# Even and odd blocks in place of first and second half in a block-Toeplitz convolution, with one PSUM pool for both of its steps

## The chip, the core and the metric

The kernel runs on one core of a Trainium2 chip. The metric is the device time of one execution in microseconds. Three executions of the kernel before are at hand; their median is 13,579.16 us. About 0.2% (27 us) is what a measurement of this kernel can tell from no change.

## The reference, cut to what matters

Two layers with residuals on x of 32 images, 128 channels and 32 x 32 pixels. The change lies in the first layer, in the part between the encoder and the first Gelu:

```python
u = _gn(x).reshape(Bsz, S, L)                       # B=32, S=128, L=1024
h = jnp.einsum('bdl,de->ble', u, W_enc) + b_enc     # 1024 hidden channels
...
K = 2.0 * jnp.einsum('dn,dnl->dl', Cc * Bd, vand).real     # 64 taps a channel
z = jnp.swapaxes(h, 1, 2)
y = jnp.fft.irfft(jnp.fft.rfft(z, n=n_fft) * jnp.fft.rfft(K, n=n_fft), n=n_fft)[..., :L]
y = y + D[:, None] * z
y = jax.nn.gelu(jnp.swapaxes(y, 1, 2))
...
```

So each of 1024 channels of each image is convolved along its 1024 positions with its own 64 taps, causally; the skip term D goes into tap 0. What follows (a gated linear unit, a layer norm, a decoder, then a deformable convolution as the second layer) is computed by a main block that the change leaves alone.

## The kernel before, in words

Four steps run one after the other: a table of the taps (`ssm_kernel_table`), the convolution (`ssm_convolution`), the main block, and a rare fallback. The main block takes some 12.1 ms of the 13.6. Everything here is in `ssm_convolution`, which ends at about 1450 us of the profile.

The convolution runs as eight passes `k`, each over 128 hidden channels: first `encode(k)`, then `convolve(k, z)`. Within them the instructions of each engine run in the order in which the program writes them (`tc.manual_schedule()`, L343), so the order of the Python statements is the order of each engine's queue.

*Encode.* For each of the 32 images, `image(b, u)` (L218) multiplies the image's eight blocks of 128 positions with 128 columns of `W_enc` (L223). Four blocks make a group `g`, and fill one tile of one PSUM bank from the pool `psz`, which has two tiles (L203). VectorE adds the bias and writes the result as `z[g]` (L227), with the block `j` and the image `b` innermost, so that 4 blocks x 32 images are 128 columns. Group 0 holds blocks 0 to 3, group 1 blocks 4 to 7, each in the order `ORDER` = 0, 2, 1, 3. In pass 0 the images come from x and go through a group norm in five steps (`group_norm_steps`, L161 to L180), whose two small matmuls (L170, L175) write into one tile of the pool `psy`; the normalised images are stored to `u_d`. In later passes they are loaded from there (L236; 512 KB each, five buffers).

*Convolve.* It goes over 16 groups of eight channels (`CG`). Each loads a Toeplitz table `toe` of 192 columns a channel (L281, 768 KB, three buffers, on SyncE's queue). For `q` in 0 and 1 (four channels each) and for `i` in 0 and 1 (the group of blocks) a tile of two banks is taken from `psy`, which has three (L204), and four matmuls fill it (L299). Each gives 192 columns a channel: 128 belong to a block itself, and 64 (`RW`) are the overlap that belongs to the next block. ScalarE copies the overlaps out of PSUM (L307, tile `t`). VectorE adds them to the blocks that they belong to (`carry`, L311): in the order 0, 2, 1, 3 the overlap of blocks 0 and 2 goes onto 1 and 3 (64 partitions), that of block 1 onto 2 (32 partitions), and in the second group that of block 3 onto block 4 (32 partitions, from the tile `last` of the first group). That is two additions for the first group and three for the second.

The Gelu of a tile (L320) is not issued at once. It is put on a list `waiting`, and `finish()` (L271) issues what is on the list after the copy and the additions of the tile that follows. The order on ScalarE is therefore: copy of tile n, Gelu of tile n-1, copy of tile n+1, Gelu of tile n. The Gelu is the last to read a tile and so lets it go. It writes `yo` (six buffers, two a group of channels). After both `q` the eight stores of a group of channels go onto the same list (L332): 128 KB each, issued on GpSimd's queue.

[...]

Of the kernel before, what the change touches and what calls it, by code (L numbers as in the profile page):

```python
# [7 lines left out]
F32 = mybir.dt.float32  # L8
AF = mybir.ActivationFunctionType
# [5 lines left out]
P = 128  # L15
# [10 lines left out]
TW = 192  # L26
# [3 lines left out]
CG = 8  # L30
# [130 lines left out]
def group_norm_steps(nc, pool, pm, gavg, eps, xt, out):  # L161


    s = pool.tile([P, 1], F32, tag="gn_s", name="gn_s")
    nm = pool.tile([P, 1], F32, tag="gn_m", name="gn_m")
    ss = pool.tile([P, 1], F32, tag="gn_ss", name="gn_ss")
    r = pool.tile([P, 1], F32, tag="gn_r", name="gn_r")
    nc.scalar.activation(out, xt, AF.Identity, accum_out=s)
    yield
    nc.tensor.matmul(pm[:, 0:1], gavg, s, start=True, stop=True)  # L170
    yield
    nc.scalar.mul(nm, pm[:, 0:1], -1.0)
    nc.scalar.activation(out, xt, AF.Square, bias=nm, accum_out=ss)
    yield
    nc.tensor.matmul(pm[:, 1:2], gavg, ss, start=True, stop=True)  # L175
    yield
    nc.scalar.activation(r, pm[:, 1:2], AF.Sqrt, bias=eps)
    nc.vector.reciprocal(r, r)
    nc.vector.tensor_scalar(out, xt, nm, r, op0=ALU.add, op1=ALU.mult)
    yield  # L180


def ssm_convolution(nc, tc, const, ins, x, u_d, kp_d, y_d):
# [12 lines left out]
    with tc.tile_pool(name="cvt", bufs=3) as tp, tc.tile_pool(  # L196
        name="cvz", bufs=1
    ) as zp, tc.tile_pool(name="cv1", bufs=1) as one, tc.tile_pool(
        name="cvu", bufs=5
    ) as up, tc.tile_pool(name="cvy", bufs=6) as yp, tc.tile_pool(  # L200
        name="cvg", bufs=4
    ) as gp, tc.tile_pool(
        name="cv_psz", bufs=2, space=PSUM  # L203
    ) as psz, tc.tile_pool(name="cv_psy", bufs=3, space=PSUM) as psy:  # L204
        w_enc = one.tile([P, D], F32, tag="w_enc", name="w_enc")
        nc.sync.dma_start(w_enc, ins["W_enc"])
        b_enc = one.tile([P, D], F32, tag="b_enc", name="b_enc")
        nc.sync.dma_start(b_enc, ins["b_enc_row"].to_broadcast([P, D]))

        def encode(k):  # L210

            z = [
                pool.tile([P, P, NB, B], F32, tag=f"z{g}", name=f"z_{k}_{g}")
                for g, pool in enumerate((one, zp))
            ]
            bias = b_enc[:, k * P : (k + 1) * P]

            def image(b, u):  # L218
                for g in range(2):
                    ps = psz.tile([P, NB, P], F32, tag="ps", name=f"psz_{k}_{b}_{g}")  # L220
                    for j in range(NB):
                        lo = (NB * g + ORDER[j]) * P
                        nc.tensor.matmul(  # L223
                            ps[:, j, :], u[:, lo : lo + P], w_enc[:, k * P : (k + 1) * P],
                            start=True, stop=True,
                        )
                    nc.vector.tensor_add(  # L227
                        z[g][:, :, :, b].rearrange("p d j -> p j d"),
                        ps,
                        bias[:, None, :].to_broadcast([P, NB, P]),  # L230
                    )

            if k > 0:
                for b in range(B):
                    u = up.tile([P, L], F32, tag="u", name=f"u_{k}_{b}")
                    nc.sync.dma_start(u, u_d[b])  # L236
                    image(b, u)
                return z


            running = {}

            def step(b):
                if b in running:
                    next(running[b][1])

            for t in range(B + 3):
                step(t - 2)
                if t - 2 in running:
                    nc.scalar.dma_start(u_d[t - 2], running[t - 2][0])  # L250
                step(t - 1)
                if t < B:
                    u = up.tile([P, L], F32, tag="u", name=f"u_{k}_{t}")
                    xt = yp.tile([P, L], F32, tag="yo", name=f"xt_{t}")
                    nc.sync.dma_start(xt, x[t])
                    pm = psy.tile([P, 2, 512], F32, tag="ps", name=f"gn_ps_{t}")
                    running[t] = u, group_norm_steps(
                        nc, gp, pm[:, 0, :2], const["gavg"], const["eps"], xt, u
                    )
                    step(t)  # L260
                if t >= 3:
                    image(t - 3, running.pop(t - 3)[0])
                step(t - 1)
                step(t)
            return z

        def convolve(k, z):
            rows = [t.rearrange("p d j b -> p d (j b)") for t in z]
            waiting = []

            def finish():  # L271
                for work in waiting:
                    work()
                waiting.clear()

            for g in range(P // CG):
                d0 = k * P + g * CG
                toe = tp.tile([P, CG, TW], F32, tag="toe", name=f"toe_{d0}")
                table = kp_d[d0 : d0 + CG, 0:TW]

                nc.sync.dma_start(  # L281
                    toe,
                    bass.AP(
                        tensor=table.tensor,
                        offset=table.offset,
                        ap=[[1, P], [KPW, CG], [1, TW]],
                    ),
                )
                yo = [
                    yp.tile([P, CG, P], F32, tag="yo", name=f"yo_{d0}_{i}") for i in range(2)  # L290
                ]
                for q in range(CG // QC):
                    c0 = q * QC
                    last = None
                    for i in range(2):
                        ps = psy.tile([P, 2, 512], F32, tag="ps", name=f"psy_{d0}_{q}_{i}")
                        ps = ps[:, :, : 2 * TW].rearrange("p h (c n) -> p h c n", c=2)
                        for c in range(QC):
                            nc.tensor.matmul(  # L299
                                ps[:, c // 2, c % 2, :],  # L300
                                rows[i][:, g * CG + c0 + c, :],
                                toe[:, c0 + c, :],
                                start=True,
                                stop=True,
                            )
                        over = tp.tile([P, 2, 2, RW], F32, tag=f"t{i}", name=f"t_{d0}_{q}_{i}")
                        nc.scalar.copy(over, ps[:, :, :, :RW])  # L307

                        def carry(to, rows, src):
                            own = ps[to : to + rows, :, :, P:TW]  # L310
                            nc.vector.tensor_add(own, own, src)  # L311

                        carry(64, 64, over[0:64])
                        carry(32, 32, over[64:96])
                        if i > 0:
                            carry(0, 32, last[96:P])
                        finish()

                        def gelu(to=yo[i][:, c0 : c0 + QC, :], ps=ps):
                            nc.scalar.activation(  # L320
                                to.rearrange("p (h c) l -> p h c l", c=2),
                                ps[:, :, :, RW:TW][:, :, :, ::-1],
                                AF.Gelu_apprx_tanh,
                            )

                        waiting.append(gelu)
                        last = over

                def store(yo=yo, d0=d0):
                    for i in range(2):  # L330
                        for j in range(NB):
                            nc.gpsimd.dma_start(  # L332
                                y_d[d0 : d0 + CG, :, i * NB + ORDER[j], :].rearrange(
                                    "d b l -> b d l"
                                ),
                                yo[i][j * B : (j + 1) * B],
                            )

                waiting.append(store)
            finish()  # L340


        with tc.manual_schedule():  # L343
            for k in range(KD):
                convolve(k, encode(k))


def deformable_general(nc, tc, const, ins, x1_d, out, image):
# [7 lines left out]
    with tc.tile_pool(name="gdf1", bufs=1) as one, tc.tile_pool(  # L356
# [27 lines left out]
        def prepare(b):  # L384
# [2 lines left out]
            nc.sync.dma_start(xt, x1_d[bass.ds(image, 1)].rearrange("o c l -> (o c) l"))  # L387
            v = one.tile([P, L], F32, tag="v", name=f"gen_dv_{b}")
            pm = psum.tile([P, 2], F32, tag="gn_ps", name="gn_ps")
            for _ in group_norm_steps(nc, one, pm, const["gavg"], const["eps"], xt, v):  # L390
                pass

            vT = two.tile([P, NCHUNK, C], F32, tag="vT", name=f"gen_dvT_{b}")
# [924 lines left out]
```

## Time and profile before

| what | value |
|---|---|
| median of three runs | 13,579.16 us (13,577.97 to 13,587.48) |
| span of the profiled execution | 13,587.2 us |
| its own time | 13,587.48 us, if it is the longest of the three, which stands 0.3 us over the span |
| TensorE busy in the span | 13,106.8 us, 96% |
| VectorE, ScalarE, GpSimd busy | 8,781.8 (65%), 3,291.8 (24%), 9,080.3 us (67%) |
| encode of pass 0 | 31 to 178 us |
| encode, passes 1 to 7 | 74.1 to 75.9 us each |
| convolve, passes 0 to 7 | 91.2 to 95.3 us each |
| first matmul of the main block's loop | 1491 us |

The profile is one execution on the chip. A row of a timeline has a start and a length in us, an engine, a line of the kernel, an operation, and what it writes and reads; `x16` means that 16 instructions are merged, and a bracket at the end tells how long the engine sat idle before and what released it. A row of waits tells who waited for whom, with the us in total, the number of times and the longest. PE is TensorE's matmul and PEld its weight load; DVE is VectorE, ACT ScalarE, POOL GpSimd and SP SyncE; PSUM tiles appear by name (`psz` in encode, `psy` in convolve). One fp32 matmul leaves two records.

### The profile page before, as it was taken

How to read it: one execution, taken by the hardware profiler on the slowest of the kernel's cores; microseconds unless marked ns; L12 is line 12 of the kernel's file. 1: busy time of each engine (PE TensorE's matmuls, PEld its weight loads, DVE VectorE, ACT ScalarE, POOL GpSimd, SP SyncE). 2: the span in 40 equal slices, each digit the busy share in tenths (PEclk: the TensorE clock that was granted, in tenths of full speed). 3: DMA queues.
4: the chain of work that ended last, by engine and by line, in shares of the span. 5: the costliest groups of instructions: out<-in, count | busy, mean ns of one | idle time of the engine just before them, and what ended most of it. 6: DMA issues, size and time to landing. Idle time of an engine off the chain costs nothing.

```text
span 13587.2 us, 133930 instructions
## 1 busy us (share of the span) xinstructions
PE 13106.8 (96%) x40482; PEld 7248.5 (53%) x40482; DVE 8781.8 (65%) x12685; ACT 3291.8 (24%) x4767; POOL 9080.3 (67%) x8868
## 2 busy tenths in 40 slices
PE   7999899999999999999999999999999999999975
PEld 7888545555555555555555555555555555555533
DVE  7787226666666666666666666666666666666677
ACT  4333222222211122222222211112222222221145
POOL 2444227777777777777777777777777777777778
PEclk9999999999999999999999999999999999999988
DMA  7888428888888888888889888888888888988876
GB/s 244 275 277 273 132 90 231 234 239 236 231 227 231 233 235 238 238 236 232 230 234 239 235 229 229 231 232 237 238 237 236 232 230 235 240 235 231 230 198 175
DMA packets 1715626, 3105.77 MB, mean 229 GB/s; under 512 B 308306, under 2 KB 1018322, under 8 KB 1713874
## 3 DMA queue, kind: packets, MB, share of 16 engines
q1 hardware_dynamic: 1502290, 2641.91, 73.2%
q10 hardware_dynamic: 163456, 320.92, 6.6%
q0 software_dynamic: 49152, 134.28, 2.9%
q8 instruction: 329, 5.39, 0.2%
q14 instruction: 399, 3.27, 0.1%
HBM read 2630.36 MB, written 466.06 MB: 228 GB/s over the span
## 4 chain that ended last, share of the span: by engine, by line
PE 81%; DMA 9%; DVE 4%; ACT 2%; POOL 2%; issue 1%; SPq 1%; ACTq 0%; DVEq 0%; POOLq 0%
PE gpv L780 24%; PE gpg L757 23%; PE dps L1091 23%; DMA ds<-dhat 4%; PE gph L796 3%; PE gpo L685 3%; PE psy L299 3%; PE psz L223 2%; DMA y_d<-yo 2%; DMA dhat<-dh 2%; DVE z L227 1%; DVE ds L1048 1%; DMA dhy<-dhat 1%; POOL y_d L332 1%; ACT ds L1040 0%
## 5 line engine op out<-in xcount | busy, mean ns | idle before, releaser
L1094 DVE TENSOR_TENSOR dp<-dps,k_weight_slots 128x256 f32<-128x256 f32 (+17 forms) x6528 | 3087.1, 483 | 3109.5 <-PE dps L1091 2914.8
L1091 PE MATMUL dps<-ds,dxw 128*128 128x256 f32 (+18 forms) x13056 | 4701.1, 447 | 223.5 <-DVE ds L1048 177.5
L1116 POOL TENSOR_TENSOR dacc<-dacc,dp 128x256 f32<-128x256 f32 (+3 forms) x4736 | 4417.4, 933 | 396.5 <-DVE dp L1111 26.6
L1091 PEld LDWEIGHTS dps<-ds,dxw 128*128 128x128 f32 x13056 | 2472.7, 192 | 3203.6 <-issue 2537.5
L757 PE MATMUL gpg<-gy,g_w_glu 128*128 128x512 f32 x8192 | 3986.4, 593 | 23.5 <-DMA gy<-y_d 15.7
L780 PE MATMUL gpv<-gy,g_w_glu 128*128 128x512 f32 x8192 | 3975.7, 592 | 0.0
L1111 POOL TENSOR_TENSOR dp<-dp 128x448 f32<-128x448 f32 (+2 forms) x2142 | 2675.1, 1249 | 1882.1 <-DVE dp L1094 1879.4
L1048 DVE TENSOR_TENSOR ds<-ds,dhy 128x1024 f32<-128x1024 f32 (+3 forms) x2176 | 3148.6, 1447 | 762.4 <-DMA ds<-dhat 647.9
L757 PEld LDWEIGHTS gpg<-gy,g_w_glu 128*128 128x128 f32 x8192 | 1546.9, 190 | 1235.8 <-issue 964.9
L780 PEld LDWEIGHTS gpv<-gy,g_w_glu 128*128 128x128 f32 x8192 | 1551.7, 190 | 1155.3 <-issue 913.8
L818 POOL TENSOR_TENSOR gs<-gs,gq 128x512 f32<-128x512 f32 x448 | 628.5, 1403 | 1341.3 <-ACT gq L817 1341.3
L817 ACT ACTIVATE gq<-gr 128x512 f32<-128x512 f32 x448 | 282.3, 630 | 4673.6 <-DVE gr L809 4611.2
L332 POOL DMA_DIRECT2D y_d<-yo x1024 | 590.1, 583 | 869.7 <-ACT yo L320 699.2
L764 ACT ACTIVATE gs<-gpg,k_b_glu 128x512 f32<-128x512 f32 x512 | 351.8, 687 | 2488.0 <-PE gpg L757 2377.6
L953 ACT ACTIVATE dh<-dr,k_minus 128x624 f32<-128x624 f32 x768 | 621.7, 809 | 642.5 <-DMA dhat<-dh 563.1
L299 PE MATMUL psy<-toe,z 128*128 128x192 f32 x4096 | 704.7, 333 | 45.2 <-ACT yo L320 43.8
L299 PEld LDWEIGHTS psy<-toe,z 128*128 128x128 f32 x4096 | 667.5, 192 | 81.6 <-ACT yo L320 74.5
L311 DVE TENSOR_TENSOR psy<-psy,t 32x256 f32<-32x256 f32 (+1 forms) x1280 | 553.7, 433 | 204.7 <-ACT t L307 162.6
L788 DVE SCALAR_TENSOR_TENSOR gs<-gpv,k_b_glu,gs 128x512 f32<-128x512 f32 x512 | 379.7, 742 | 437.3 <-PE gpv L780 437.2
L687 POOL TENSOR_TENSOR gs<-gs,gr 128x512 f32<-128x512 f32 x448 | 634.7, 1417 | 0.0
L954 ACT ACTIVATE dh<-dh,one 128x624 f32<-128x624 f32 x768 | 626.3, 815 | 25.0
L223 PE MATMUL psz<-w_enc,u 128*128 128x128 f32 x4096 | 568.6, 293 | 44.9 <-DVE z L227 32.3
(162 smaller groups left out, 6052.4 us busy)
## 6 DMA issues: line engine op xcount, KB each, us to landing
dhy<-dhat SPq DMA_DIRECT2D x1536, 512.0 KB
ds<-dhat SPq DMA_DIRECT2D x1440, 512.0 KB
dhat<-dh ACTq DMA_DIRECT2D x768, 312.0 KB
y_d<-yo POOLq DMA_DIRECT2D x1024, 128.0 KB, 5.4
gy<-y_d SPq DMA_DIRECT2D x512, 256.0 KB
u<-u_d SPq DMA_DIRECT2D x224, 512.0 KB
toe<-kp_d SPq DMA_DIRECT2D x128, 768.0 KB
dxw<-dvt_d SPq DMA_DIRECT2D x1248, 64.0 KB
```

The costliest lines, as they stand in the source:

```text
L223: nc.tensor.matmul(ps[:, j, :], u[:, lo : lo + P], w_enc[:, k * P : (k + 1) * P], start=True, stop=True,)
L299: nc.tensor.matmul(ps[:, c // 2, c % 2, :], rows[i][:, g * CG + c0 + c, :], toe[:, c0 + c, :], start=True, stop=True,)
L332: nc.gpsimd.dma_start(y_d[d0 : d0 + CG, :, i * NB + ORDER[j], :].rearrange("d b l -> b d l"), yo[i][j * B : (j + 1) * B],)
L687: nc.gpsimd.tensor_add(sums[0], sums[0], r)
L757: nc.tensor.matmul(gate, w_glu[:, k, D + m * P : D + m * P + P], ys[k], start=(k == 0), stop=(k == KD - 1),)
L780: nc.tensor.matmul(val, w_glu[:, k, m * P : m * P + P], ys[k], start=(k == 0), stop=(k == KD - 1),)
L818: nc.gpsimd.tensor_add(sums[1], sums[1], sq)
L1048: nc.vector.tensor_mul(s[:, :m], s[:, :m], hy[:, :m])
L1091: nc.tensor.matmul(ps, xw[:, j, :], s[:, :m, :, y0 : y0 + ny], start=True, stop=True)
L1094: nc.vector.tensor_mul(prod[:, :m, :, y0 : y0 + ny], ps, w[:, :, :, None].to_broadcast([P, m, KY2, ny]),)
L1111: adder.tensor_add(prod[:, :m, 0], prod[:, :m, 0], prod[:, :m, 1])
L1116: nc.gpsimd.tensor_add(to, to, prod[:, slot : slot + nj, 0])
```

## The change

Group 0 now holds the even blocks (0, 4, 2, 6) and group 1 the odd ones (1, 5, 3, 7): block number `2 * ORDER[j] + g`. In that order the overlap of every even block belongs to the odd block in the same place, so one addition over 128 partitions carries all four; the overlaps of blocks 1 and 5 go onto 2 and 6 (64 partitions) and that of block 3 onto 4 (32 partitions). That is three additions for both groups in place of five. They can be issued only when both tiles of a `q` have been filled and copied, so copies, additions, `finish()` and Gelus now go by pairs of tiles: both copies, three additions, and then the two Gelus of the pair before. The stores use the new block numbers.

The two PSUM pools become one of four tiles of two banks. An image of encode takes one tile and uses both banks; each of the two statistics of the group norm takes a tile of its own; a pair of convolve takes two.

```diff
-    ) as gp, tc.tile_pool(
-        name="cv_psz", bufs=2, space=PSUM
-    ) as psz, tc.tile_pool(name="cv_psy", bufs=3, space=PSUM) as psy:
+    ) as gp, tc.tile_pool(name="cv_ps", bufs=4, space=PSUM) as psum:
+
+        def banks(name):
+            return psum.tile([P, 2, 512], F32, tag="ps", name=name)
...
+        def block(g, j):
+
+            return 2 * ORDER[j] + g
...
             def image(b, u):
+                both = banks(f"psz_{k}_{b}")
                 for g in range(2):
-                    ps = psz.tile([P, NB, P], F32, tag="ps", name=f"psz_{k}_{b}_{g}")
+                    ps = both[:, g].rearrange("p (j d) -> p j d", j=NB)
                     for j in range(NB):
-                        lo = (NB * g + ORDER[j]) * P
+                        lo = block(g, j) * P
...
-                    pm = psy.tile([P, 2, 512], F32, tag="ps", name=f"gn_ps_{t}")
+
+                    def pm(n, t=t):
+                        return banks(f"gn_ps_{t}_{n}")[:, 0, 0:1]
...
-                    last = None
+                    out, over = [], []
                     for i in range(2):
-                        ps = psy.tile([P, 2, 512], F32, tag="ps", name=f"psy_{d0}_{q}_{i}")
+                        ps = banks(f"psy_{d0}_{q}_{i}")
...
-                        over = tp.tile([P, 2, 2, RW], F32, tag=f"t{i}", name=f"t_{d0}_{q}_{i}")
-                        nc.scalar.copy(over, ps[:, :, :, :RW])
-
-                        def carry(to, rows, src):
-                            own = ps[to : to + rows, :, :, P:TW]
-                            nc.vector.tensor_add(own, own, src)
-
-                        carry(64, 64, over[0:64])
-                        carry(32, 32, over[64:96])
-                        if i > 0:
-                            carry(0, 32, last[96:P])
-                        finish()
-
-                        def gelu(to=yo[i][:, c0 : c0 + QC, :], ps=ps):
+                        t = tp.tile([P, 2, 2, RW], F32, tag=f"t{i}", name=f"t_{d0}_{q}_{i}")
+                        nc.scalar.copy(t, ps[:, :, :, :RW])
+                        out.append(ps)
+                        over.append(t)
+
+                    def carry(to, rows, ps, src):
+                        own = ps[to : to + rows, :, :, P:TW]
+                        nc.vector.tensor_add(own, own, src)
+
+                    carry(0, P, out[1], over[0])
+                    carry(64, 64, out[0], over[1][0:64])
+                    carry(32, 32, out[0], over[1][64:96])
+                    finish()
+
+                    def gelu(yo=yo, c0=c0, out=out):
+                        for to, ps in zip(yo, out):
                             nc.scalar.activation(
-                                to.rearrange("p (h c) l -> p h c l", c=2),
+                                to[:, c0 : c0 + QC, :].rearrange(
+                                    "p (h c) l -> p h c l", c=2
+                                ),
                                 ps[:, :, :, RW:TW][:, :, :, ::-1],
                                 AF.Gelu_apprx_tanh,
                             )
 
-                        waiting.append(gelu)
-                        last = over
+                    waiting.append(gelu)
...
-                                y_d[d0 : d0 + CG, :, i * NB + ORDER[j], :].rearrange(
+                                y_d[d0 : d0 + CG, :, block(i, j), :].rearrange(
```

More of the change, by code (lines that the diff above doesn't have):

```diff
@@ L169, in group_norm_steps @@
     yield
-    nc.tensor.matmul(pm[:, 0:1], gavg, s, start=True, stop=True)
+    p = pm(0)
+    nc.tensor.matmul(p, gavg, s, start=True, stop=True)
     yield
-    nc.scalar.mul(nm, pm[:, 0:1], -1.0)
+    nc.scalar.mul(nm, p, -1.0)
     nc.scalar.activation(out, xt, AF.Square, bias=nm, accum_out=ss)
     yield
-    nc.tensor.matmul(pm[:, 1:2], gavg, ss, start=True, stop=True)
+    p = pm(1)
+    nc.tensor.matmul(p, gavg, ss, start=True, stop=True)
     yield
-    nc.scalar.activation(r, pm[:, 1:2], AF.Sqrt, bias=eps)
+    nc.scalar.activation(r, p, AF.Sqrt, bias=eps)
     nc.vector.reciprocal(r, r)
@@ L255, in encode @@
                     nc.sync.dma_start(xt, x[t])
-                    pm = psy.tile([P, 2, 512], F32, tag="ps", name=f"gn_ps_{t}")
+                    def pm(n, t=t):
+                        return banks(f"gn_ps_{t}_{n}")[:, 0, 0:1]
                     running[t] = u, group_norm_steps(
-                        nc, gp, pm[:, 0, :2], const["gavg"], const["eps"], xt, u
+                        nc, gp, pm, const["gavg"], const["eps"], xt, u
                     )
@@ L389, in prepare @@
             pm = psum.tile([P, 2], F32, tag="gn_ps", name="gn_ps")
-            for _ in group_norm_steps(nc, one, pm, const["gavg"], const["eps"], xt, v):
+            for _ in group_norm_steps(
+                nc, one, lambda n: pm[:, n : n + 1], const["gavg"], const["eps"], xt, v
+            ):
                 pass
```

## The prediction

> **What bounds the kernel now.** I read the page first: TensorE is busy for 96% of the span and the chain that ended last is mostly TensorE. The diff touches only the first stage, though, so I read that stage by itself. Its lines are L223/L227 (encode) and L299/L307/L311/L320/L332 (convolve); they end at 1450 us. The table of stretches cuts it into its parts (columns: stretch, its length, busy us and instructions of PE, PEld, DVE, ACT, POOL, then granted clock, DMA share, GB/s):
>
> ```profile
> 272.00:347.50 75.50, 67.19 (x514) 60.83 (x514) 64.11 (x68) 1.96 (x4) 10.85 (x19) 1.00 0.81 261
> 347.50:440.50 93.00, 88.36 (x513) 84.15 (x514) 68.52 (x158) 55.81 (x125) 64.56 (x113) 0.98 0.90 294
> ```
>
> An encode pass takes about 75 us, a convolve pass about 93 us; there are eight of each, and both are near the bound of TensorE (67 of 75.5 busy, 88 of 93). Next the waits between 178 and 1450 us say what TensorE waits for:
>
> ```profile
> PEld psz L223 <- DVE z L227: 86.0, 242, 2.6
> PEld psy L299 <- ACT yo L320: 74.5, 125, 4.0
> PE psy L299 <- ACT yo L320: 43.8, 32, 3.7
> ACT yo L320 <- DMA y_d<-yo: 51.6, 34, 3.9
> PE psz L223 <- DVE z L227: 31.8, 110, 2.4
> ```
>
> Both are waits for a PSUM tile to come free: in encode VectorE's addition must have read it, in convolve ScalarE's Gelu. Some of the Gelus in turn wait for an output buffer that a store still reads. The timeline of an undisturbed stretch of convolve shows the order that matters:
>
> ```profile
> 389.59 0.37 ACT L307 COPY t<-psy 128x256 f32<-128x256 f32 x1 [0.44 <-PE psy L299]
> 390.08 0.60 ACT L320 ACTIVATE yo<-psy 128x512 f32<-128x512 f32 x1
> 390.73 2.41 PEld L299 LDWEIGHTS psy<-toe,z 128*128 128x128 f32 x15 [0.23 <-ACT yo L320]
> 390.89 0.37 ACT L307 COPY t<-psy 128x256 f32<-128x256 f32 x1 [0.21 <-PE psy L299]
> 391.16 0.60 ACT L320 ACTIVATE yo<-psy 128x512 f32<-128x512 f32 x1
> ```
>
> A copy of the tile just filled, then the Gelu of the tile before it. TensorE needs that Gelu's tile only one tile later (three tiles), so it loses 0.23 us in every four tiles (5.41 us). In encode, each image costs 2.29 us, with both sides waiting in turn on two one-bank tiles:
>
> ```profile
> 301.65 2.07 PE L223 MATMUL psz<-w_enc,u 128*128 128x128 f32 x16 [0.22 <-DVE z L227]
> 302.84 1.96 DVE L227 TENSOR_TENSOR z<-psz,b_enc 128x512 f32<-128x512 f32 x2 [0.34 <-PE psz L223]
> 303.93 2.08 PE L223 MATMUL psz<-w_enc,u 128*128 128x128 f32 x16 [0.22 <-DVE z L227]
> ```
>
> [...]
>
> [...] copies and Gelus run in program order, a Gelu starting only after the copy ahead of it although its data is older. [...] here the Gelu starts 0.27 us after a copy of 0.37 (391.16 against 390.89), 0.10 of overlap. [...] of the two L227 additions below, each about 1.03 us long, the second starts 0.86 after the first. [...]
>
> ```profile
> 171.00 1.89 DVE L227 TENSOR_TENSOR z<-psz,b_enc 128x512 f32<-128x512 f32 x2
> ```
>
> **The change part by part.** I subtract and add against the profiled execution. Its span is 13,587.2 us, the longest of the three listed times is 13,587.48, and I take that for its own; it is 0.06% above the median of 13,579. The sum below is a difference, which I put on the median.
>
> *Convolve: the Gelu now stands behind two copies.* Per pair of tiles (even, odd) the program order on ScalarE becomes copy even, copy odd, and then, after `finish()`, the two Gelus of the pair before. Four tiles are two pairs, so the next pair's first matmul needs the tile that the first of these Gelus frees. That Gelu stands in the queue behind copy odd, and copy odd waits until TensorE has finished the odd tile. TensorE cannot run ahead: from the end of one pair to the start of the next it sits through a copy and a Gelu. Worked out from an undisturbed cycle. In the pattern above TensorE fills a tile in (5.41 - 0.23)/4 = 1.30 us. A pair takes 16 records at 0.1625, with 0.10 more behind a first record that waited; the last starts 2.54 us after the first, and its own 0.33 ends at 2.87. The copy starts 0.09 later (2.96), the Gelu 0.27 after it (3.23), lasts 0.60 (3.83), and TensorE follows after 0.05: **3.88 us per pair** against 2.70 now. The queue behind the waiting matmul is the whole next pair on TensorE, and the copies on ScalarE wait for that. The second tile's Gelu ends 0.6 after the first's, inside the 1.30 that the first tile takes, so it costs nothing.
>
> A pass has 32 pairs. The first two find free tiles; 30 starts of pairs and the next encode's first image wait. So a pass is 31 x 3.88 + 2.7 = 122.9 us. The eight passes of before, from the first L299 record to the next stage's first, are 94.1, 93.0, 94.9, 91.2, 94.5, 92.4, 95.3 and 92.2, sum 747.6. After: 8 x 122.9 = 983. Difference **+236 us**. The stall is 3.88 - 2.60 = 1.28 us, of which copy and Gelu are 0.87 and drain and handovers 0.41. The Gelu cannot pass the copy, so a gain is excluded; if the handovers differ by some 0.12 us either way, the 248 stalls make -30 or +30 us.
>
> This already takes in that today's stalls for stores go: a pass at 32 x 2.70 would be 86.6 us, so 93.4 - 86.6 = 7 us a pass are waits for `y_d` stores while DMA is busy at 0.90. With 7.8 us instead of 5.4 per group of eight channels DMA falls to some 0.65 and these waits vanish; they are replaced, not added.
>
> *Convolve: three additions instead of five.* L311 runs 1280 times at 433 ns; 512 go, 222 us of VectorE. But VectorE is no bound in convolve (five at 0.46 us is 2.3 of 2.70 per pair), and Gelus of the pair before never wait for it once they stand a pair behind. **0 us.** The cover is the stall itself: without it a pair's additions (1.4 us) still fit beside 2.6 us of matmuls. Whether an addition over 128 partitions costs more than one over 64 isn't shown; 32 and 64 cost the same (0.43), and even twice that hides.
>
> *Stores.* Eight issues a group on POOL at 0.58 us, 4.7 us, now in 7.8 us; other block numbers, same sizes, all issued behind the first pair of the next group instead of its first tile. The output buffers are six, three groups, 23 us, against 5.4 us to landing. **0.** The table loads on SP keep their order; 0.
>
> *Encode: four tiles of two banks.* TensorE can now be three images ahead, so the ping-pong goes and the slower of two engines sets the pace. TensorE: from the first image of a pass, where it isn't held, 16 records take 1.95 us, so (1.95 - 0.27)/15 = 0.112 each, 1.79 an image, and with 0.02 at each bank change 1.83. VectorE: 2 x 0.86 = 1.72. DMA: an image is 512 KB; in an encode stretch (300 to 345 us) the loads' queue takes 76.5% of the engines at 2.29 us an image, 1.75 us. So 1.83: 32 x 1.83 = 58.6, with 1 us at the ends 59.5 a pass. Seven passes before: 75.4, 74.2, 74.3, 75.9, 74.2, 74.4, 74.1, sum 522.5 (at their starts they also lose 1 to 2 us on the two tiles). After 416.5: **-106 us**. Bounds: if an addition really costs its 1.04 us, 67.5 a pass and -50; at 57 a pass -123. The loads of an image have four image times, 7.3 us, from buffer to use; today their last packets land 3 to 5 us after the issue.
>
> *The first pass with the group norm.* Its two statistics now take tiles of the same rotation, three tiles an iteration of 4.3 us, so a tile returns after 5.7 us and was read within one iteration. In this stretch TensorE waits for ScalarE and the normalisation, for the old tiles 0.4 us in all. **0**, bounds -2 and +10.
>
> *The seam to the main block.* From 1450 to 1491 us constants and weights load; the backlog of stores there is about 2.4 MB today and will be shorter: **-4 us**, 0 to -8. The main block itself isn't touched.
>
> Sum: 236 + 0 + 0 - 106 + 0 - 4 = +126 us, 13,579 + 126 = **13,705 us**.
>
> **Rivals.**
> 1. *Encode stays bound by VectorE* at 1.04 us an addition. For it: all its records are that long. Against it: the pair of 1.89 us. 13,705 + 56 = 13,761.
> 2. *The wait for the Gelu doesn't hold TensorE*, so four tiles do what their number suggests. One mechanism: the Gelu of the pair before is through ahead of copy odd. Then a pair takes 2.6 us, a pass 84, convolve 672 (-76), with encode and seam -110: 13,579 - 186 = 13,393. It decides from the point where convolve loses less than those 110 us: (748 + 110)/8 = 107 us a pass, a pair of 3.37 us, a stall of 0.77. Against it: the queue order; the copy alone starts 0.09 after TensorE has ended. Faster than before if true.
> 3. *Nothing visible*: the stall is there, but near 0.77 us, and encode pays for it. That needs all but 0.36 us of copy and Gelu to be hidden, with the handovers as they are; 13,579.
>
> **How the numbers follow.** My forecast 0.76, range 13,660 to 13,750 (stall ±30, encode and seam some ±15); rival 1 0.16; rival 2 0.04; rival 3 0.04. Both leading cases are slower. The range 13,645 to 13,785 holds the forecast and rival 1 with its own ±25. Faster by over 0.2% (27 us, about what a measurement of this kernel can tell from no change) 0.04, within 0.2% 0.03, slower 0.93.
>
> **What would show it.** In the timeline of convolve each pair's first matmul should start 0.05 us after a Gelu, with a gap of about 1.0 us on TensorE in every 3.9; waits of "psy" for "yo" should be some 250 us in all; "yo for DMA" close to none; a convolve pass 123 us, DMA share 0.65 to 0.7. An encode pass should be 59 to 60 us with VectorE's and TensorE's mutual waits gone. The additions should be 768. It's wrong if Gelus of a pair start before its successor's second copy, if the pair's period is under 3.5 us, or if encode stays above 65.

## The result, and where the time went

| | before | changed |
|---|---|---|
| median of all runs | 13,583.3 us (4 runs) | 14,082.4 us (4 runs, 14,077.2 to 14,084.8) |
| ratio | 1 | 1.0364, 95% interval 1.0349 to 1.0379 |
| span of the profiled execution | 13,587.2 us | 14,075.5 us |
| encode of pass 0 ends | 178.0 us | 203.5 us |
| encode, passes 1 to 7 | 522.5 us (74.6 a pass) | 735.7 us (105.1 a pass) |
| convolve, passes 0 to 7 | 747.6 us (93.4 a pass) | 990.8 us (123.9 a pass) |
| end of convolve's last matmul to the main block's first | 43.1 us | 44.1 us |
| from there to the end | 12,096 us | 12,101 us |

The change costs 499 us, where +126 was forecast. The spans differ by 488: 25.5 in the first encode pass, 213 in the other seven, 243 in convolve, and 6 elsewhere. Convolve lost what was forecast. Encode lost twice what it should have won.

The table of stretches of the changed kernel, for one encode and one convolve pass (columns as in the prediction):

```profile
330.20:435.30 105.10, 68.50 (x513) 62.11 (x514) 61.26 (x65) 1.47 (x3) 6.70 (x12) 0.97 0.55 175
435.30:558.90 123.60, 91.51 (x515) 82.24 (x513) 41.99 (x96) 54.14 (x126) 68.08 (x119) 1.00 0.79 228
```

TensorE works about as long as before in both (67 and 88 us there) and now idles beside it, in encode for 37 of 105 us. VectorE and DMA are no fuller (61 of 105 us, DMA at 0.55): nothing in encode is near a bound, so it is a chain of waits. They stand in the list of waits from 203 to 1930 us (in all, how often, the longest):

```profile
PEld psy L311 <- ACT yo L334: 320.8, 240, 2.7
DVE z L236 <- PE psz L232: 309.0, 246, 2.2
PEld psz L232 <- DVE z L236: 300.8, 231, 1.4
PE psz L232 <- DVE z L236: 256.1, 231, 1.1
PE psy L311 <- ACT yo L334: 250.0, 240, 2.4
...
POOL y_d L347 <- DMA y_d<-yo: 1.9, 4, 0.7
```

TensorE waits 250 us for Gelus (44 before), which is the stall that was forecast, and the waits of Gelus for stores are gone from the list, as forecast (GpSimd's own, the last line, were 105 us before). But it also waits 256 us for encode's additions (32 before), and the additions wait 309 us for it. The timeline of encode shows how:

```profile
599.77 2.05 PE L232 MATMUL psz<-w_enc,u 128*128 128x128 f32 x16 [1.10 <-DVE z L236]
...
600.97 1.91 DVE L236 TENSOR_TENSOR z<-psz,b_enc 128x512 f32<-128x512 f32 x2 [1.25 <-PE psz L232]
602.93 1.86 PEld L232 LDWEIGHTS psz<-w_enc,u 128*128 128x128 f32 x16 [1.30 <-DVE z L236]
602.93 2.05 PE L232 MATMUL psz<-w_enc,u 128*128 128x128 f32 x16 [1.11 <-DVE z L236]
604.13 1.92 DVE L236 TENSOR_TENSOR z<-psz,b_enc 128x512 f32<-128x512 f32 x2 [1.25 <-PE psz L232]
```

Each group of 16 records (encode's 2,048 matmuls left 4,096 in all) is the odd half of one image and the even half of the next. Then TensorE stands still for 1.11 us until VectorE has added the bias to that even half, and only then does it fill the odd half beside it. The period is 602.93 - 599.77 = 3.16 us an image, against 2.29 before. In convolve the pattern is as it was worked out:

```profile
472.19 0.37 ACT L319 COPY t<-psy 128x256 f32<-128x256 f32 x1 [0.93 <-PE psy L311]
472.46 1.10 ACT L334 ACTIVATE yo<-psy 128x512 f32<-128x512 f32 x2
472.59 1.35 DVE L325 TENSOR_TENSOR psy<-psy,t 128x256 f32<-128x256 f32 x3 [2.54 <-ACT t L319]
473.11 2.57 PEld L311 LDWEIGHTS psy<-toe,z 128*128 128x128 f32 x16 [1.31 <-ACT yo L334]
473.11 2.87 PE L311 MATMUL psy<-toe,z 128*128 128x192 f32 x16 [1.02 <-ACT yo L334]
```

The second copy of a pair, 0.27 us later the two Gelus of the pair before, and 0.05 us after the first of these (472.46 + 0.60) TensorE's next pair. Pairs follow each other at 3.89 us.

### The profile page after: what moved, and what is told of

It reads as the page before. It is cut to its first block, busy times and chain, and to the rows that moved or that the text cites. A ratio compares the mean times of both kernels' runs of the same rounds, so it can differ in the third digit from the quotient of the medians.

```text
span 14075.5 us, 133449 instructions
## 1 busy us (share of the span) xinstructions
PE 13142.1 (93%) x40482; PEld 7242.3 (51%) x40482; DVE 8545.7 (61%) x12173; ACT 3285.3 (23%) x4767; POOL 9073.0 (64%) x8868
## 4 chain that ended last, share of the span: by engine, by line
PE 81%; DMA 8%; DVE 5%; ACT 3%; issue 1%; POOL 1%; SPq 1%; ACTq 0%; DVEq 0%; POOLq 0%
PE gpv L797 23%; PE gpg L774 23%; PE dps L1108 22%; DMA ds<-dhat 4%; PE psy L311 4%; DVE z L236 3%; PE gph L813 3%; PE gpo L702 3%; PE psz L232 3%; DMA dhat<-dh 1%; ACT yo L334 1%; DMA y_d<-yo 1%; DMA dhy<-dhat 1%; DVE ds L1065 1%; ACT ds L1057 1%
## 5 line engine op out<-in xcount | busy, mean ns | idle before, releaser
L311 PE MATMUL psy<-toe,z 128*128 128x192 f32 x4096 | 733.7, 333 | 250.0 <-ACT yo L334 250.0
L325 DVE TENSOR_TENSOR psy<-psy,t 128x256 f32<-128x256 f32 (+2 forms) x768 | 333.7, 434 | 654.9 <-ACT t L319 642.6
L236 DVE TENSOR_TENSOR z<-psz,b_enc 128x512 f32<-128x512 f32 x512 | 496.7, 1028 | 379.4 <-PE psz L232 374.2
L232 PEld LDWEIGHTS psz<-w_enc,u 128*128 128x128 f32 x4096 | 529.6, 208 | 365.0 <-DVE z L236 355.8
```

The costliest lines, as they stand in the source:

```text
L232: nc.tensor.matmul(ps[:, j, :], u[:, lo : lo + P], w_enc[:, k * P : (k + 1) * P], start=True, stop=True,)
L236: nc.vector.tensor_add(z[g][:, :, :, b].rearrange("p d j -> p j d"), ps, bias[:, None, :].to_broadcast([P, NB, P]),)
L311: nc.tensor.matmul(ps[:, c // 2, c % 2, :], rows[i][:, g * CG + c0 + c, :], toe[:, c0 + c, :], start=True, stop=True,)
```

## The theory after the result, and its rivals

The two halves of an image share one tile. The program issues the even half's matmuls, the addition that reads them, then the odd half's matmuls into the same tile; these wait for the addition, 1.11 us an image, although they write another bank. Before, each half had its own tile, so there was nothing to wait for but the tile's return (0.22 us an image). The list of waits above counts TensorE's wait 231 times, and the seven passes have 7 x 32 = 224 odd halves. The prediction went by the order of instructions in convolve and not in encode.

Rivals: the two banks of one tile cannot be written and read side by side without loss; the order matmuls, addition, matmuls, addition serialises, whoever owns the tile; or four tiles in one rotation are too few. For convolve the rival to the order on ScalarE is likewise that four tiles are too few for pairs.

## Experiments

Each is the changed kernel with the edit shown, unless it says otherwise. The times of the stages come from each run's trace (from the first matmul of one stage to that of the next, the last convolve pass to the end of its own last matmul); "pass 0" is the time at which the first encode pass ends. Each row is one profile. Stages of the same code differ between rows by up to 5 us in pass 0 and 2 us a pass in encode (changed and e3) and by 1 us a pass in convolve (e5 and e8), so smaller differences say nothing.

| run | whole | pass 0 | encode, mean of 1 to 7 | convolve, mean of 0 to 7 |
|---|---|---|---|---|
| before | 13,583 | 178.0 | 74.6 | 93.4 |
| changed | 14,082 | 203.5 | 105.1 | 123.9 |
| matmuls first (e1) | 13,744 | 190.5 | 61.0 | 123.8 |
| a tile per half (e2) | 13,729 | 177.0 | 61.4 | 123.8 |
| Gelu between the copies (e3) | 13,845 | 208.9 | 107.3 | 92.9 |
| e1 and e3 together (e4) | 13,512 | 187.9 | 62.5 | 92.8 |
| old halves, one pool, matmuls first (e5) | 13,490 | 186.7 | 61.0 | 91.5 |
| e2 and e3, even tile's additions first (e6) | 13,512 | 177.4 | 65.0 | 92.7 |
| e4 with half the tables (e7) | 13,470 | 189.6 | 61.9 | 88.6 |
| e5 with two tiles in pass 0 (e8) | 13,486 | 177.8 | 61.1 | 92.5 |

**e1: all matmuls of an image first.**

```diff
                 both = banks(f"psz_{k}_{b}")
-                for g in range(2):
-                    ps = both[:, g].rearrange("p (j d) -> p j d", j=NB)
+                halves = [both[:, g].rearrange("p (j d) -> p j d", j=NB) for g in range(2)]
+                for g, ps in enumerate(halves):
                     for j in range(NB):
...
+                for g, ps in enumerate(halves):
                     nc.vector.tensor_add(
```

> The changed kernel with one edit in encode: all eight matmuls of an image come first, then both additions. Theory (one tile for both halves: the addition on the even half stands between the two halves' matmuls, and the odd half's matmuls wait for it): the wait goes, TensorE runs ahead over four tiles, an encode pass falls from 105 us to 59 to 67 us, convolve stays at 123.6, the whole is 14,082 - 7 x 43 - 25 = about 13,755 us. Rival A (TensorE writing one bank of a tile beside VectorE's read of the other is slow in itself): the waits may go, but a pass stays above 75 us. Rival B (the rotation over four tiles comes round late): unchanged at 105.

Measured: 13,743.9 us, ratio to before 1.0121 (1.0106 to 1.0137); 61.0 us an encode pass, convolve unchanged. A stretch of the timeline has no wait left in it:

```profile
344.51 10.88 DVE L237 TENSOR_TENSOR z<-psz,b_enc 128x512 f32<-128x512 f32 x12
344.83 10.44 PE L232 MATMUL psz<-w_enc,u 128*128 128x128 f32 x92
```

92 records in 10.44 us, less the last one's own 0.27, are 0.112 each, 1.79 us an image, and the additions follow at 0.90 us. So the wait was the cause, and the figures with which encode had been forecast (59.5 us) hold as soon as it is gone. Rival B falls, since the rotation is the same. Rival A falls as a cause: in the changed kernel the odd half's matmuls start only when the addition has ended (600.97 + 1.91 = 602.88, then 602.93), so they are late and not slow (16 records in 2.05 us, 2.07 before). What it says of one tile's two banks stays untested, since in e1 too the additions start only after all 16 records of their tile.

**e2: a tile for each half, the order left alone.**

```diff
-                both = banks(f"psz_{k}_{b}")
                 for g in range(2):
-                    ps = both[:, g].rearrange("p (j d) -> p j d", j=NB)
+                    own = banks(f"psz_{k}_{b}_{g}")
+                    ps = own[:, 0].rearrange("p (j d) -> p j d", j=NB)
```

> The changed kernel with encode's order left as it is, but each half of an image in a tile of its own, whose second bank stays unused. Theory (the shared tile makes the odd half wait): as good as putting the matmuls first, 59 to 67 us a pass, about 13,755 us in all. Rival (what counts is the order matmuls, addition, matmuls, addition, whoever owns the tile): 105 us a pass, 14,080 us.

Measured: 13,729.5 us (one run), 61.4 us a pass. TensorE runs through here too:

```profile
344.73 10.44 PE L232 MATMUL psz<-w_enc,u 128*128 128x128 f32 x92
344.82 10.88 DVE L236 TENSOR_TENSOR z<-psz,b_enc 128x512 f32<-128x512 f32 x12
```

The order alone does no harm, and e1 shows the same of the shared tile alone. Either repair is enough, so the cause is the two together: an addition on one half of a tile, issued ahead of the matmuls into its other half. Pass 0 too is back at 177 us, while e1 leaves it at 190; e8 takes that up.

**e3: the first Gelu of the pair before between the two copies.**

```diff
                         out.append(ps)
                         over.append(t)
+                        if i > 0:
+                            finish()
+                        elif waiting:
+                            waiting.pop(0)()
...
                     carry(32, 32, out[0], over[1][64:96])
-                    finish()
-
-                    def gelu(yo=yo, c0=c0, out=out):
-                        for to, ps in zip(yo, out):
+
+                    for to, ps in zip(yo, out):
+
+                        def gelu(to=to, c0=c0, ps=ps):
...
-                    waiting.append(gelu)
+                        waiting.append(gelu)
```

> The changed kernel with one edit in convolve: of the two Gelus of the pair before, the first is issued between the two copies of a pair, the second behind them. Theory (TensorE's stall in convolve is the Gelu that stands behind the second copy): it has a tile's time to run, the pair goes from 3.89 us to 2.6 to 2.8 us, a pass from 123.6 to 84 to 93 us (the lower end if the stores keep up), encode stays at 105, in all 14,082 - 8 x 35 = about 13,800 us. Rival (four tiles are too few for pairs, whatever the order on ScalarE): a pass stays above 110 us.

Measured: 13,845.3 us, ratio to before 1.0193 (1.0177 to 1.0209); convolve is back at 92.9 us a pass, encode took 107.3 with the stall left in it. The stall in convolve was the place of the Gelu in ScalarE's queue; four tiles are enough for pairs. The table of stretches, a convolve and an encode pass:

```profile
208.90:305.40 96.50, 89.87 (x514) 85.00 (x512) 41.46 (x94) 57.12 (x125) 63.22 (x110) 0.97 0.87 280
305.40:411.00 105.60, 68.29 (x513) 61.84 (x513) 61.77 (x66) 1.96 (x5) 10.68 (x19) 0.97 0.56 183
```

The first row stands again near the bound of TensorE (89.9 of 96.5) and with DMA at 0.87, the second as in the changed kernel.

**e4: both edits.**

> Both edits: matmuls first in encode, the first Gelu between the copies in convolve. If the two stalls are all that the change costs and they don't meet: encode 59 to 67 us a pass, convolve 84 to 93, in all 13,583 - 7 x 12 - 8 x 4 = about 13,465 us, below the kernel before (13,583). If DMA is the next bound (0.90 busy in convolve before), convolve stays at 93 and the whole is about 13,495. Rival (the gain of the one is given back in the other): 13,583.

Measured: 13,512.0 us, ratio 0.9951 (0.9938 to 0.9965). The two stalls are all that the change costs, and they add: e1 takes away 338 us, e3 237, both 570. The version is faster than the kernel before, by less than the first expectation, since convolve stays at 92.8 us a pass: the second, DMA as the next bound, is nearer (its share is 0.89 from 188 to 281 us, in the first convolve pass). In the waits of its convolve TensorE waits for Gelus, and some of these for stores:

```profile
PEld psy L312 <- ACT yo L339: 77.4, 166, 2.3
ACT yo L339 <- DMA y_d<-yo: 56.4, 50, 2.4
PE psy L312 <- ACT yo L339: 36.9, 43, 2.0
```

**e7: half the table loads left out of e4.** The odd groups of channels use the table of the group before them.

```diff
-                toe = tp.tile([P, CG, TW], F32, tag="toe", name=f"toe_{d0}")
+                if g % 2 == 0:
+                    toe = tp.tile([P, CG, TW], F32, tag="toe", name=f"toe_{d0}")
...
```

> The mended version (both edits), but the Toeplitz table is loaded only for every second group of channels and used twice; the odd groups are computed with the wrong taps, 64 of 128 loads of 768 KB are left out. If DMA is what holds convolve at 92 to 94 us a pass (through output buffers that wait for their stores), a pass falls to 84 to 88 us and the Gelus' waits for stores go from 56 us to under 10; 13,512 - 8 x 6 = about 13,465 us. Rival (the order on ScalarE and VectorE bounds it): a pass stays at 92 or more.

Measured: 13,470.4 us (one run); convolve 88.6 us a pass, and the Gelus' waits for output buffers fall from 56 to 20 us:

```profile
PEld psy L313 <- ACT yo L340: 43.2, 135, 3.0
...
ACT yo L340 <- DMA y_d<-yo: 20.1, 17, 3.1
```

So 4 of the 9 us between 92.8 and TensorE's own 84 (as in the prediction's rival 2) went with half of the table loads, which points to DMA traffic. The waits fell by less than expected, to 20 and not under 10, and a pass ended just above what was expected; the other 5 us are not accounted for.

**e5: the pool alone.** The kernel before with the one pool of four tiles and e1's order in encode; the halves, the five additions and the Gelu behind each copy are the old ones.

```diff
-            return 2 * ORDER[j] + g
+            return NB * g + ORDER[j]
...
```

> The kernel before with one part of the change alone: the pool of four tiles of two banks, with all matmuls of an image first; first and second halves, five additions and a Gelu behind each tile's copy stay as before. If the gain of the mended version (13,512 us) is all in encode, this one gives the same: encode 61 to 63 us a pass, convolve 91 to 95, 13,500 to 13,525. Rival: the three additions over even and odd blocks bring something of their own (VectorE has 222 us less to do): then this one is slower than 13,512 by more than 25 us.

Measured: 13,490.4 us, ratio 0.9932 (0.9918 to 0.9945), the median 22 us under e4, and the two intervals overlap. Three additions in place of five bring nothing that shows: convolve is 91.5 us a pass with five and 92.8 with three. The order of the blocks brings encode nothing either (61.0 us a pass in e1 and here). What the change has to give is nearly all in encode: of 105 us between the spans its seven passes give 95 and convolve 16, and pass 0 takes 9 back.

**e6: the additions onto the even tile first, and a tile per half.**

```diff
-                    carry(0, P, out[1], over[0])
                     carry(64, 64, out[0], over[1][0:64])
                     carry(32, 32, out[0], over[1][64:96])
+                    carry(0, P, out[1], over[0])
```

> Even and odd blocks, the first Gelu between the copies, a tile for each half of an image, and the two additions onto the even tile issued ahead of the one onto the odd tile. Pass 0 should end at 177 us in place of 188 (as in the run with a tile per half), encode at 61 to 63 a pass, and the 0.23 us that TensorE still waits in each group of convolve should go, since the first Gelu waits for two additions and no longer for three. If nothing else bounds convolve: 13,512 - 11 - 8 x 3.7 = about 13,470 us. If DMA bounds it (0.90 busy before), convolve stays at 92 to 93 a pass and only pass 0 gains: about 13,500.

Measured: 13,512.3 us, ratio 0.9949 (0.9935 to 0.9963), the same as e4. ScalarE's timeline shows the edit at work and what takes its gain:

```profile
522.09 0.37 ACT L319 COPY t<-psy 128x256 f32<-128x256 f32 x1 [0.43 <-PE psy L311]
522.36 0.60 ACT L338 ACTIVATE yo<-psy 128x512 f32<-128x512 f32 x1
523.39 0.37 ACT L319 COPY t<-psy 128x256 f32<-128x256 f32 x1 [0.43 <-PE psy L311]
...
524.69 0.37 ACT L319 COPY t<-psy 128x256 f32<-128x256 f32 x1 [0.43 <-PE psy L311]
...
525.99 0.37 ACT L319 COPY t<-psy 128x256 f32<-128x256 f32 x1 [0.43 <-PE psy L311]
...
531.81 0.37 ACT L319 COPY t<-psy 128x256 f32<-128x256 f32 x1 [0.43 <-PE psy L311]
532.88 0.60 ACT L338 ACTIVATE yo<-psy 128x512 f32<-128x512 f32 x1 [0.70 <-DMA y_d<-yo]
```

Copies now follow each other at 1.30 us without the 0.23 between groups, until a Gelu finds its output buffer still being stored (0.70). A convolve pass is 92.7 us as before. Pass 0 gained its 10 us. Encode took 65.0 us a pass, against 61 to 63 expected: in the first of the seven passes the first four images take 5.3, 5.1, 3.4 and 2.1 us before it settles at 1.79. TensorE waits for additions there, and its granted clock is down: from 278.9 to 282.9 us it was 0.50, with records 0.21 us apart in place of 0.112 (the changed kernel too has 0.21 us a record from 104.95 to 107.00 us, at a granted clock of 0.50). The clock was halved like this for 7 to 10 us in five of the seven passes, which took 64.9 to 66.3 us; the two without it took 62.5 and 63.3. In e2, with the same encode, it was halved in two passes (62.1 and 63.1 us) and not in the other five (60.9). From these means the clock makes up an estimated 1.6 of the 3.6 us between e6 and e2 (65.0 - 62.9 less 61.4 - 60.9). Why it fell more often here, and what the other 2 us are, stays open.

**e8: e5 with a tile per half in pass 0.**

```diff
-                halves = [both[:, g].rearrange("p (j d) -> p j d", j=NB) for g in range(2)]
+                other = both[:, 1] if k > 0 else banks(f"psz_{k}_{b}_1")[:, 0]
+                halves = [t.rearrange("p (j d) -> p j d", j=NB) for t in (both[:, 0], other)]
```

> The version with the old halves and one pool, and in pass 0 alone a tile for each half of an image, so that four tiles are taken in every iteration (two for the image, two for the statistics) and each kind meets its own tiles again. Theory for pass 0 (with three tiles an iteration a statistic's matmul gets the tile of an image and must wait for its additions): pass 0 ends at 177 us in place of 187, the rest is unchanged, 13,480 us. Rival (pass 0 is later because TensorE does eight matmuls of an image before it comes to the statistics): it stays at 187, 13,490 us.

Measured: 13,485.5 us, ratio 0.9927 (0.9913 to 0.9940). Pass 0 ends at 177.8 in place of 186.7 us, so with four tiles an iteration the first pass costs no more than before. That fits the theory of the rotation, but the edit gives each half its own release as well, and no run tells these two apart. The whole gained only 5 us: convolve took 740 us in place of 732, and it lies between 732 and 744 us in all versions without the stall (e3 to e6, e8). e8 and e5 are the fastest versions tried that leave nothing out, 0.7% below the kernel before. More output buffers, which would touch the stores' waits, were not tried.

## Why the prediction was wrong, point by point

- **Convolve, the Gelu behind two copies: right.** Forecast 3.88 us a pair and +236 us; measured 3.89 and +243 (3 us of the rest are in the first pass, which took 126.6 us). e3 shows that this is the place of the Gelu in the queue; ScalarE ran all 512 copies and 512 Gelus of the changed kernel in the order of the program. The rival in which the Gelu doesn't hold TensorE falls.
- **Today's waits for stores go, and are replaced: right.** They fall from 52 us to none in the list, and come back in e3 to e6 as soon as the stall is mended. DMA stood at 0.76 to 0.80 in a pass, above the 0.65 to 0.7 of the forecast.
- **Three additions instead of five at 0: right,** and e5 shows it. 128 partitions take no longer (0.43 us, against 0.43 on 32 and 0.44 on 64).
- **Encode, "TensorE can now be three images ahead, so the ping-pong goes": wrong, and most of the error.** Forecast -106 us, measured +213: 319 of the 373 us by which the sum missed. The step counted tiles and forgot the order within one: the odd half's matmuls wait for the addition on the even half of the same tile. It costs 3.16 us an image in place of 1.83. The figures themselves (0.112 a record, 0.86 to 0.90 between additions) held: with the wait gone, e1 measures 61.0 us a pass against 59.5. In the changed kernel too TensorE's next bank was another than the one being read, and it waited 1.11 us an image; in e1 and e2 it runs at 0.112 us a record, as in an unheld stretch before, beside additions that read other tiles. The wait that cost the time goes by tile: in the same order of instructions an image takes 3.16 us with one tile for both halves and 1.79 with two (e2).
- **The first pass with the group norm at 0: wrong by 25 us.** The same wait makes up half of it (e1: 190.5 us), the other half goes with a tile per half (e2: 177.0).
- **The seam at -4: no gain.** It took 44.1 us in place of 43.1.
- **The rivals.** Encode bound by VectorE at 1.04 us an addition would have cost 56 us; e1 excludes it. None of the rivals, and no end of the range, had encode slower than before. I had bounded this part by engines' rates alone, which cannot show a chain.

## What to carry to other kernels

Count not only how many tiles a rotation has, but what is issued between two writes into the same one: a reader of the first half, issued ahead of the second half's writes, turned a two-bank tile into a serial chain here, however many tiles lay free. Issue all writes of a tile before its first reader (e1, 61.0 us a pass in place of 105.1), or give each part a tile of its own (e2, 61.4). When an operation is moved behind another in one engine's queue, ask what the other one waits for: here one Gelu, moved from behind one copy to behind two, cost 30 us a pass, and putting it back between them returned all of that.

## What the runs showed of the hardware

VectorE's additions of 128x512 last 1.01 to 1.07 us by their records, yet twelve of them take 10.88 us in e1, (10.88 - 1.03)/11 = 0.90 us from one start to the next; the length of a record is not the rate there. In that stretch the 0.90 is TensorE's pace, half of 1.79 us an image. An addition on 128 partitions takes as long as on 32 or 64 (0.43 to 0.44 us for 256 elements), so joining additions over partitions saves VectorE's time: 768 of them took 334 us in the changed kernel, 1,280 took 554 before. Here others did not wait for it, and e5 shows no gain.
